# Running sums in two fp32r passes, ternary weights partly on ScalarE, gate steps on GpSimd, and new planner times

## The chip, the cores and the metric

The kernel runs on one core of one Trainium2 chip. The metric is the device time of one execution in microseconds. A core has TensorE (PE), VectorE (DVE), ScalarE (ACT), GpSimd (POOL) and a queue engine, SyncE (SP), which issues the DMAs here. Each engine executes its own instructions in order and waits on semaphores of the others.

## What is computed

Sixteen sequences of 256 tokens of width 256 pass through two layers; after each of the four steps stands `layernorm(x + step(x))`.

```python
# step 1: per head (16 heads of 16), Fourier transforms of q and kv, normalized,
#         kv summed up along the sequence
q, kv = x @ W_q.T, x @ W_kv.T
qf, kvf = l2norm(fft(q)), l2norm(fft(kv))
values = ifft(qf * cumsum(kvf, axis=sequence)).real @ W_o.T
# step 2: 8 experts; a gate per token picks one
x_diff = (x - mean_diff) / norm
score = (select_weight . x_diff)**2 summed over 8
gate = sigmoid(slope * (score - center)); scale = gate.max(); idx = gate.argmax()
mod = bias[idx] + degen[idx] @ (update[idx] . (x - debias[idx]))
out = (1 - scale) * x + scale * mod
# step 3: softmax attention, 16 heads of 16, W_qkv and W_o
# step 4: ternary weights, width 1024
def _ternary_weight(w, group_size):          # group_size = 64
    wb = w.astype(jnp.bfloat16)
    wg = wb.reshape(-1, group_size)
    scale = jnp.clip(jnp.mean(jnp.abs(wg), axis=-1, keepdims=True), 1e-08, None)
    q = jnp.clip(jnp.round(wg / scale), -1.0, 1.0)
    ...
h = square(relu(x @ ternary(W_fc).T)); out = rms_norm(h) @ ternary(W_proj).T
```

## The kernel before

The work is recorded first and ordered afterwards. Helpers `pe`, `dve`, `act`, `pool` and `op` (SP) record an operation with the tiles that it writes and reads, a cost in microseconds and a priority (`order.prio`, a virtual time: lower goes first). `Order.run` is a list scheduler: it keeps a clock for each engine, takes the engine whose next operation could start first, and of its operations that could start within `SLACK` of that the one with the lowest priority. Tiles get their buffers at that moment, so costs and priorities decide the order on every engine and which buffer is used when. `pin` fixes the order found. A DMA issue holds its queue for `ISSUE`.

The pieces of work are these.

- **Prologue.** `warm` and `fold_in` (L447, L459) prepare PE and the folded weights `wf`; `centred` (L505, L511) centres two weights on ScalarE; `fold_out` (L475 to L496) prepares `gi`, `ge`, `r0`, `r0b`.
- **front(b, early)**, steps 1 and 2 of sequence b, 16 times; sequences 0 to 3 are early. Projection (L645), squares and copies on ScalarE (L652, L653), sums (L656), an inverse root by three Newton steps on GpSimd (L664 to L667, four operations each), scaling (L671), transposes of q (L685) with a ScalarE copy (L689), the running sum of kv as a product with the triangle `tri` (L693, L694, output `cu`), products on VectorE (L700 to L702 early, L721 to L738 later), the inverse transform (L711 early, L747 later), layernorm (L586 to L599), transposes (L572, copied by L371 or L372), the gate's inputs (L768, L770, L779), and the gate: small operations of 16 columns, L792 to L809, in a chain over VectorE with the exponential on ScalarE (L798). `mk` (L812) is transposed (L823, L826) and multiplied with `dg` (L831); L838 and `layernorm_of_centred` (squares L612, root on GpSimd L580 and L581, scaling L617 or L620) give x2, whose transposes (L572) are copied to x2T.
- **ternaries()**: eight tiles of 128x512. Each is loaded, cast to bf16 (L526), reduced to sums of magnitudes per group of 64 (L527), and turned into signs times scale (L528 to L535, four of them 512 columns wide), all on VectorE but the cast; PE transposes it (L540) and a copy puts it in `w1T` or `w2T`. The tiles are held in `oT` and `o`, which the attention needs later (`terned`).
- **attention(i)**, step 3 for sequences 4i to 4i + 3 together, four times. Projections (L869) need x2T of all four; VectorE transposes them into `zt` (L878); some go to DRAM (L887) and back as `v` (L907). For 16 heads scores (L935) and their negated maxima (L944), transposed (L948, L949) and written back as a row (L952). Then, head by head, scores again (L974), exponentials (L983), values (L989), and for each pair of heads L997 to L1001 into `o`. Then transposes of `o` (L1018), the output product (L1032), sum (L1040) and layernorm.
- **back(b, late)**, step 4: transposes (L1054, L1057), split into high and low parts in fp32r (L1058), the first product (L1068), relu and squares (L1077 to L1086), split (L1090, L1092), the second product (L1100), norm (L1111, L1115), L1121, layernorm and the store.

The priorities interleave them: attention i stands around 100(i + 1), its maxima from -60 on, its heads from -10 on, 7 apart; fronts of the next group from 30 on, 15 apart; backs of the last group from 30 on, 20 apart. The last group's backs come at the end. An fp32 matmul stands in the trace as two records, an fp32r one as one.

## Time and profile before

| | |
|---|---|
| median of 3 runs | 754.0 us (742.52, 754.22, 754.0) |
| profiled execution | 740.27 us, of which the span of instructions is 738.5 |
| mean granted TensorE clock | 0.954 |
| PE, VectorE busy | 707.9, 619.4 us |
| ScalarE, GpSimd busy | 432.5, 186.3 us |
| first projection of an attention (L869) | at 87.4 us |

A profile line gives the line of the code, engine, operation, output and inputs with their shapes, the number of instructions, then busy time, mean time of one in ns, and idle time of the engine in front of them with what ended it. The records of one engine may overlap: the next operation starts before the last one's record ends, so the spacing of starts, not the length of a record, is what an operation costs in a row of them.

### The profile page before, as it was taken

What the parts mean: (1) busy time and instruction counts of PE and PEld (TensorE: products, weight loads), DVE (VectorE), ACT (ScalarE), POOL (GpSimd) and SP (SyncE); (2) the same over time, 40 slices, a digit from 0 to 9 for tenths busy, and PEclk for the clock granted to TensorE, in tenths of its full rate; (3) what the DMA queues carried; (4) which work ended last, traced back from release to release, by engine and by line L of the source; (5) the groups of instructions that cost most, each with busy time, mean ns of one, the idle gap of its engine ahead of it and who ended that gap; (6) DMA issues with size and microseconds to landing.
All of it is one profiled execution on the core that took longest, in us unless ns stands there. A gap on an engine that the chain in (4) does not pass through costs nothing.

```text
span 738.5 us, 15139 instructions
## 1 busy us (share of the span) xinstructions
PE 707.9 (96%) x5664; PEld 503.1 (68%) x5664; DVE 619.4 (84%) x1391; ACT 432.5 (59%) x929; POOL 186.3 (25%) x482
## 2 busy tenths in 40 slices
PE   9999898999999999999999999999989999999994
PEld 6687455765668567767755668787665677865993
DVE  2999997998788999899989879899559958784786
ACT  4436411344677246888571417879951278877883
POOL 3752011032415003335360014121110001120143
PEclk9999996798999999999999989999999989999996
DMA  9100102700101154010111403000001430000000
GB/s 292 64 30 30 28 11 73 60 23 8 32 16 29 32 81 59 16 36 21 34 45 33 64 3 31 1 17 16 17 15 30 69 31 16 17 17 16 1 30 29
DMA packets 86957, 27.16 MB, mean 37 GB/s; under 512 B 67996, under 2 KB 84196, under 8 KB 86884
## 3 DMA queue, kind: packets, MB, share of 16 engines
q1 hardware_dynamic: 86884, 26.20, 16.7%
q8 instruction: 44, 0.72, 0.4%
q14 instruction: 29, 0.24, 0.1%
HBM read 16.76 MB, written 8.91 MB: 35 GB/s over the span
## 4 chain that ended last, share of the span: by engine, by line
PE 70%; DVE 18%; POOL 4%; ACT 3%; issue 3%; DMA 1%; DVEq 0%; ACTq 0%
PE bank L869 10%; PE bank L935 9%; PE bank L989 8%; PE bank L974 8%; PE bank L1100 6%; PE bank L1068 6%; PE bank L645 5%; PE bank L1032 4%; DVE nm L944 4%; PE bank L747 2%; PE bank L572 2%; PE bank L831 2%; PE bank L693 1%; PE bank L770 1%; DVE zt L878 1%
## 5 line engine op out<-in xcount | busy, mean ns | idle before, releaser
L983 ACT ACTIVATE zt<-bank 128x512 f32<-128x512 f32 x256 | 134.3, 596 | 57.6 <-PE bank L974 45.3
L944 DVE TENSOR_REDUCE nm<-bank 128x2 f32<-128x512 f32 x256 | 158.3, 677 | 10.7 <-PE bank L935 10.4
L580 POOL TENSOR_SCALAR st<-st 128x2 f32<-128x2 f32 x80 | 24.3, 304 | 402.8 <-DVE st L1115 153.4
L869 PE MATMUL bank<-wqr,x2T 128*128 128x512 f32 (+1 forms) x256 | 91.8, 508 | 1.0 <-DVE nm L944 1.0
L935 PE MATMUL bank<-zt 16*128 16x256 f32 x1024 | 83.1, 424 | 1.6 <-ACT work L371 1.4
L974 PE MATMUL bank<-zt 17*128 17x256 f32 x1024 | 80.6, 409 | 1.3 <-DVE nm L944 0.7
L935 PEld LDWEIGHTS bank<-zt 16*128 16x128 f32 x1024 | 54.2, 196 | 31.5 <-issue 16.3
L869 PEld LDWEIGHTS bank<-wqr,x2T 128*128 128x128 f32 x256 | 48.5, 197 | 36.4 <-issue 28.8
L1068 PE MATMUL bank<-xs,w1T 128*128 128x256 f32 x512 | 72.5, 292 | 0.8 <-DVE xs L1058 0.5
L989 PE MATMUL bank<-zt,v 128*32 128x256 f32 x1024 | 72.7, 395 | 0.0
L878 DVE STREAM_TRANSPOSE zt<-bank 128x1024 f32<-128x1024 f32 (+1 forms) x48 | 66.5, 1462 | 7.2 <-PE bank L869 7.2
L1068 PEld LDWEIGHTS bank<-xs,w1T 128*128 128x128 f32 x512 | 65.8, 194 | 6.7 <-issue 2.7
L1100 PE MATMUL bank<-w2T,hi 128*128 128x256 f32 x256 | 69.1, 303 | 1.1 <-ACT hi L1090 0.9
L1100 PE MATMUL bank<-w2T,lo 128*128 128x256 f32 x256 | 65.5, 290 | 3.1 <-DVE lo L1092 3.1
L974 PEld LDWEIGHTS bank<-zt 17*128 17x128 f32 x1024 | 51.2, 188 | 22.0 <-issue 9.8
L581 POOL TENSOR_TENSOR st<-st,mhalf 128x2 f32<-128x2 f32 x80 | 62.5, 782 | 6.5
L645 PE MATMUL bank<-wf,x 128*128 128x512 f32 x128 | 63.2, 626 | 0.0
L371 ACT COPY work<-bank 128x512 f32<-128x512 f32 (+1 forms) x36 | 18.4, 515 | 62.3 <-PE bank L869 34.1
L1100 PEld LDWEIGHTS bank<-w2T,hi 128*128 128x128 f32 x256 | 49.7, 194 | 7.6 <-issue 3.9
L1092 DVE TENSOR_TENSOR lo<-work,hi 128x512 fp32r<-128x512 f32 x64 | 43.4, 682 | 13.1 <-ACT hi L1090 13.1
L1100 PEld LDWEIGHTS bank<-w2T,lo 128*128 128x128 f32 x256 | 49.9, 195 | 4.4 <-DVE lo L1092 4.1
L989 PEld LDWEIGHTS bank<-zt,v 128*32 128x32 f32 x1024 | 28.3, 111 | 31.9 <-issue 10.8
(205 smaller groups left out, 1261.3 us busy)
## 6 DMA issues: line engine op xcount, KB each, us to landing
x<-in_xT SPq DMA_DIRECT2D x16, 256.0 KB
v<-vd SPq DMA_DIRECT2D x32, 128.0 KB
out<-work SPq DMA_DIRECT2D x16, 256.0 KB
x<-in_x SPq DMA_DIRECT2D x12, 256.0 KB
vd<-work SPq DMA_DIRECT2D x12, 256.0 KB
vd<-work SPq DMA_DIRECT2D x12, 128.0 KB
oT<-in_wfc SPq DMA_DIRECT2D x4, 256.0 KB
o<-in_wproj SPq DMA_DIRECT2D x4, 256.0 KB
```

Of the source, the lines that this page charges most:

```text
L581: pool([dst], [dst, mhalf], 0.7, lambda: G.tensor_tensor(dst.v, dst.v, a(mhalf)[:, 0:n], ALU.pow))
L645: T.matmul(pb.v.rearrange("p a s k -> p (a s k)"), xT.v[:, c, ts(t, P)], a(wf)[:, c].rearrange("p a s f -> p (a s f)"), start=(c == 0), st ...
L869: T.matmul(b.v.rearrange("p j d -> p (j d)"), x2T.v[:, c, tb].rearrange("p g k -> p (g k)"), a(wqr)[:, c, j0 * HD : (j0 + nj) * HD], start ...
L878: lambda b=b, tb=tb, j0=j0, nj=nj: V.transpose(ztv[:, j0 : j0 + nj, ts(tb, 32)], b.v.unsqueeze(2).to_broadcast([P, nj, 2, HD])),
L935: T.matmul(sc[g].v[:, t, :], part(g, HD, 0, h, t * P, P), part(g, HD, 1, h), start=True, stop=True,)
L944: lambda nm=nm, sc=sc, g=g, k=k: V.tensor_reduce(nm.v[:, g, k, :], sc[g].v, AX.X, ALU.max, negate=True),
L974: T.matmul(sc[g].v[:, c, :], part(g, HD + 1, 1, h, c * P, P), part(g, HD + 1, 0, h), start=True, stop=True,)
L983: act([e], [sc[g]], 512, lambda e=e, sc=sc, g=g: A.activation(e.v, sc[g].v, AF.Exp, scale=HD ** -0.5))
L989: T.matmul(av.v[32 * g : 32 * g + 32, hk, :], v_part(g, h, c), es[g].v[:, c, :], start=(c == 0), stop=(c == 1),)
L1068: T.matmul(pb.v[:, i, :], a(w1T)[:, n // 2, ts(q * 2 + i, P)], xs.v[:, n % 2, n // 2, :], start=(n == 0), stop=(n == 3),)
L1092: dve([lo], [h, hi], 512, lambda h=h, hi=hi, lo=lo: V.tensor_tensor(lo.v, h.v, hi.v.bitcast(F32), ALU.subtract), us=0.63)
L1100: T.matmul(pw.v[:, t, :], part.v[:, i, ts(t, P)], a(w2T)[:, q * 2 + i, :], start=(q + t + i + n == 0), stop=(q + t + i + n == HID // P // ...
```

## The change

Line numbers behind the change are up to 22 higher.

- In later fronts the kv part is split into a high part in fp32r (`hi`, ScalarE) and the rest (`lo`, VectorE), and the running sum is the product of both with `trir`, an fp32r copy of the triangle: eight fp32r matmuls in place of four fp32 ones.
- For each ternary tile ScalarE takes magnitudes with their sums (8 operations of 64 columns), signs (512 columns) and signs times scale (8 of 64); VectorE compares magnitudes with the threshold and multiplies.
- Five gate steps go from VectorE to GpSimd in every front, a sixth in later ones.
- `ISSUE` goes from 0.43 to 0.6, the heads' spacing from 7 to 6, the backs' start from 30 to 45.

```diff
@@ -93,7 +93,7 @@
 NEAR = {PE: 0.0, DVE: 0.06, ACT: 0.06, POOL: 0.1, SP: 0.3}
 SLACK = {PE: 0.15, DVE: 0.1, ACT: 0.1, POOL: 0.1, SP: 0.0}
 SWITCH = 0.13
-ISSUE = 0.43
+ISSUE = 0.6
 MOVE = 1.2
 LATER = 15.0
 
@@ -393,10 +393,11 @@
     f0s = fixed(zt_[:, 3072:3360].rearrange("p (c f) -> p c f", c=2))
     rows = fixed(zt_[0:NE, 3360:3496])
     ge = fixed(zt_[:, 3496:4008].rearrange("p (m d) -> p m d", m=2))
-    ones, mhalf = const("ones", [P, P]), const("mhalf", [P, 2])
+    ones, mhalf, zero = const("ones", [P, P]), const("mhalf", [P, 2]), const("zero", [P, 1])
     wf = const("wf", [P, 2, 2, 2, P])
     gi = const("gi", [P, 2, D])
     r0 = const("r0", [P, 2, 136])
+    trir = fixed(place("trir", [P, S], F32R))
     r0b = const("r0b", [P, 136])
     dg = const("dg", [72, D])
     slope, center = const("slope", [P, NE]), const("center", [P, NE])
@@ -432,8 +433,10 @@
     load(lambda: a(wqr), wqkvT.rearrange("(c p) e -> p c e", p=P), wqr, prio=-8.0, size=3.0)
     load(lambda: a(wo1), wo1T.rearrange("(c p) e -> p c e", p=P), wo1, prio=-8.0)
 
+    act([trir], [small], 256, lambda: A.copy(a(trir), tri))
     dve([ones], [], P, lambda: V.memset(a(ones), 1.0))
     dve([mhalf], [], 2, lambda: V.memset(a(mhalf), -0.5))
+    dve([zero], [], 2, lambda: V.memset(a(zero), 0.0))
     va = [a(t)[:, 0 : H * GB * (HD + 1)].rearrange("p (n g d) -> p n g d", g=GB, d=HD + 1) for t in v]
     for t in v:
         pool([t], [], 1.2, lambda t=t: G.memset(a(t), 1.0))
@@ -516,7 +519,7 @@
         ng = 512 // GROUP
         w, up, dn = (tile_("tern", [P, ng, GROUP]) for _ in range(3))
         wb, sc = tile_("wb", [P, ng, GROUP]), tile_("sb", [P, ng])
-        tot, th = stat(ng), stat(2, ng)
+        tot, th, scf = stat(ng), stat(ng), stat(ng)
 
         def wide(t):
             return t.unsqueeze(2).to_broadcast([P, ng, GROUP])
@@ -524,15 +527,18 @@
         place_w = lambda: w.slot.ap if len(w_dram.shape) == 2 else w.slot.ap.rearrange("p (c f) -> p c f", c=2)
         op((SP, MOVE, lambda: nc.sync.dma_start(place_w(), w_dram)), [w], [], prio=-8.5)
         act([wb], [w], 512, lambda: A.copy(wb.v, w.v))
-        dve([tot], [wb], 512, lambda: V.tensor_reduce(tot.v, wb.v, AX.X, ALU.add, apply_absolute_value=True))
+
+        for g in range(ng):
+            act([(dn, g), (tot, g)], [wb], 76, lambda g=g: A.activation(dn.v[:, g], wb.v[:, g], AF.Abs, accum_out=tot.v[:, g : g + 1]))
+        act([up], [wb], 512, lambda: A.activation(up.v, wb.v, AF.Sign))
         dve([sc], [tot], 8, lambda: V.tensor_scalar(sc.v, tot.v, 1.0 / GROUP, TINY, ALU.mult, ALU.max))
 
-        dve([(th, 0)], [sc], 8, lambda: V.tensor_scalar(th.v[:, 0], sc.v, 257.0 / 512.0, None, ALU.mult))
-        dve([(th, 1)], [sc], 8, lambda: V.tensor_scalar(th.v[:, 1], sc.v, -257.0 / 512.0, None, ALU.mult))
-        dve([up], [wb, th], 512, lambda: V.tensor_tensor(up.v, wb.v, wide(th.v[:, 0]), ALU.is_gt), us=0.63)
-        dve([dn], [wb, th], 512, lambda: V.tensor_tensor(dn.v, wb.v, wide(th.v[:, 1]), ALU.is_lt), us=0.63)
-        dve([up], [up, dn], 512, lambda: V.tensor_tensor(up.v, up.v, dn.v, ALU.subtract), us=0.63)
-        dve([up], [up, sc], 512, lambda: V.tensor_tensor(up.v, up.v, wide(sc.v), ALU.mult), us=0.63)
+        dve([th], [sc], 8, lambda: V.tensor_scalar(th.v, sc.v, 257.0 / 512.0, None, ALU.mult))
+        dve([scf], [sc], 8, lambda: V.tensor_copy(scf.v, sc.v))
+        for g in range(ng):
+            act([(up, g)], [(up, g), scf, zero], 64, lambda g=g: A.activation(up.v[:, g], up.v[:, g], AF.Identity, bias=a(zero), scale=scf.v[:, g : g + 1]))
+        dve([dn], [dn, th], 512, lambda: V.tensor_tensor(dn.v, dn.v, wide(th.v), ALU.is_gt), us=0.63)
+        dve([up], [up, dn], 512, lambda: V.tensor_tensor(up.v, up.v, dn.v, ALU.mult), us=0.63)
         b = ps([P, 4, P], "p")
 
         def go():
@@ -679,6 +685,15 @@
 
         pq, cu = ps([P, 2, S], kind), ps([P, 2, S], kind)
 
+        kv = [] if early else [tile_("hi", [P, 2, 2, P]), tile_("lo", [P, 2, 2, P])]
+        for t in range(0 if early else 2):
+            k = lambda t=t: qk[t].v.rearrange("p a (s h) k -> p a s (h k)", s=2)[:, :, 1, :]
+            act([(kv[0], t)], [qk[t]], 256, lambda t=t, k=k: A.copy(kv[0].v[:, t], k()))
+            dve(
+                [(kv[1], t)], [qk[t], (kv[0], t)], 256,
+                lambda t=t, k=k: V.tensor_tensor(kv[1].v[:, t], k(), kv[0].v[:, t].bitcast(F32), ALU.subtract), us=0.4,
+            )
+
         def go():
             for e in range(2):
                 for t in range(2):
@@ -690,10 +705,14 @@
 
         def go():
             for e in range(2):
-                T.matmul(cu.v[:, e, :], part(0, e, 1), tri, start=True, stop=False)
-                T.matmul(cu.v[:, e, P:S], part(1, e, 1), tri[:, 0:P], start=False, stop=True)
-
-        pe([cu], [*qk, small, *extra], 1.28, go)
+                if early:
+                    T.matmul(cu.v[:, e, :], part(0, e, 1), tri, start=True, stop=False)
+                    T.matmul(cu.v[:, e, P:S], part(1, e, 1), tri[:, 0:P], start=False, stop=True)
+                for n, kn in enumerate(kv):
+                    T.matmul(cu.v[:, e, :], kn.v[:, 0, e, :], a(trir), start=(n == 0), stop=False)
+                    T.matmul(cu.v[:, e, P:S], kn.v[:, 1, e, :], a(trir)[:, 0:P], start=False, stop=(n == 1))
+
+        pe([cu], [*(qk if early else [*kv, trir]), small, *extra], 1.28 if early else 0.8, go)
         if early:
 
             one, two = w(P, 2, S), w(P, 2, S)
@@ -790,11 +809,14 @@
 
         num, z, gate, top, oh, first, keep = e16(), e16(), e16(), stat(2), e16(), stat(2), stat(2)
         dve([num], [c2], 128, lambda: V.tensor_reduce(num.v, c2.v.rearrange("p t (n s) -> p t n s", s=NR), AX.X, ALU.add))
-        dve([z], [f, x1sq], 16, lambda: V.tensor_tensor(z.v, f.v[:, :, 128:136], per_token(x1sq.v), ALU.add))
+        if early:
+            dve([z], [f, x1sq], 16, lambda: V.tensor_tensor(z.v, f.v[:, :, 128:136], per_token(x1sq.v), ALU.add))
+        else:
+            pool([z], [f, x1sq], 0.27, lambda: G.tensor_tensor(z.v, f.v[:, :, 128:136], per_token(x1sq.v), ALU.add))
         dve([z], [z], 80, lambda: V.reciprocal(z.v, z.v))
-        dve([z], [num, z], 16, lambda: V.tensor_tensor(z.v, num.v, z.v, ALU.mult))
-        dve([z], [z, center], 16, lambda: V.tensor_tensor(z.v, z.v, per_expert(a(center)), ALU.subtract))
-        dve([z], [z, slope], 16, lambda: V.tensor_tensor(z.v, z.v, per_expert(a(slope)), ALU.mult))
+        pool([z], [num, z], 0.27, lambda: G.tensor_tensor(z.v, num.v, z.v, ALU.mult))
+        pool([z], [z, center], 0.27, lambda: G.tensor_tensor(z.v, z.v, per_expert(a(center)), ALU.subtract))
+        pool([z], [z, slope], 0.27, lambda: G.tensor_tensor(z.v, z.v, per_expert(a(slope)), ALU.mult))
         act([gate], [z], 80, lambda: A.activation(gate.v, z.v, AF.Exp, scale=-1.0))
         dve([gate], [gate], 16, lambda: V.tensor_scalar(gate.v, gate.v, 1.0, None, ALU.add))
         dve([gate], [gate], 80, lambda: V.reciprocal(gate.v, gate.v))
@@ -804,9 +826,9 @@
         dve([oh], [oh, small], 16, lambda: V.tensor_tensor(oh.v, oh.v, per_expert(rev), ALU.mult))
         dve([first], [oh], 16, lambda: V.tensor_reduce(first.v, oh.v, AX.X, ALU.max))
         dve([oh], [oh, first], 16, lambda: V.tensor_tensor(oh.v, oh.v, per_token(first.v), ALU.is_equal))
-        dve([keep], [top], 2, lambda: V.tensor_scalar(keep.v, top.v, -1.0, 2.0, ALU.mult, ALU.add))
+        pool([keep], [top], 0.27, lambda: G.tensor_scalar(keep.v, top.v, -1.0, 2.0, ALU.mult, ALU.add))
         mk = tile_("mk", [P, 2, 72])
-        dve([mk], [oh, top], 16, lambda: V.tensor_tensor(mk.v[:, :, 64:72], oh.v, per_token(top.v), ALU.mult))
+        pool([mk], [oh, top], 0.27, lambda: G.tensor_tensor(mk.v[:, :, 64:72], oh.v, per_token(top.v), ALU.mult))
         dve(
             [mk], [mk, f], 128,
             lambda: V.tensor_tensor(
@@ -964,7 +986,7 @@
             for hk in range(2):
                 n = hp * 2 + hk
                 h = HEADS[n]
-                order.prio = base + -10.0 + 7.0 * n
+                order.prio = base + -10.0 + 6.0 * n
                 at = [z[q_at(h)], z[k_at(h)], turn[q_at(h)], turn[k_at(h)]]
                 sc = [ps([P, 2, S], "a") for _ in range(GB)]
 
@@ -1144,7 +1166,7 @@
         for g in range(GB):
             base = 100.0 * (i + 1)
             if i > 0:
-                order.prio = base + 30.0 + 20.0 * g
+                order.prio = base + 45.0 + 20.0 * g
                 back((i - 1) * GB + g, False)
             if i + 1 < NG:
                 order.prio = base + 30.0 + 15.0 * g
```

## The prediction

> **What bounds the kernel now.** I first read the page: busy time, slices, and the shares of the chain that ended last.
>
> ```profile
> span 738.5 us, 15139 instructions
> PE 707.9 (96%) x5664; PEld 503.1 (68%) x5664; DVE 619.4 (84%) x1391; ACT 432.5 (59%) x929; POOL 186.3 (25%) x482
> ...
> DVE  2999997998788999899989879899559958784786
> ACT  4436411344677246888571417879951278877883
> ...
> PE 70%; DVE 18%; POOL 4%; ACT 3%; issue 3%; DMA 1%; DVEq 0%; ACTq 0%
> ```
>
> PE at 96% looks like the bound, but its records overlap. The chain shows what a matmul takes when others queue behind it:
>
> ```profile
> 235.50 1.92 PE bank L1068 x16
> ...
> 54.91 1.73 PE bank L711 x8
> ```
>
> So a 256-column fp32r matmul takes 120 ns (its record says 292), and an fp32 one, which is two records, 2 x 216 = 433 ns. Counting every matmul this way gives about 602 us of PE work in the 738.5, not 708: some 18% of the span PE waits or runs below full clock. VectorE's 619 us hardly overlap, so VectorE is nearly as tight as PE. I then cut the span where the first attention's projections begin (L869 at 87.4 us), and where the last attention's values end:
>
> ```profile
> 0.00:87.40 87.40, 82.53 (x400) 60.54 (x401) 68.99 (x207) 43.29 (x102) 35.27 (x90) 0.98 0.29 94
> ...
> 87.40:678.00 590.60, 577.65 (x4930) 398.34 (x4928) 505.32 (x1092) 349.51 (x745) 133.47 (x360) 0.96 0.17 30
> 678.00:738.50 60.50, 47.67 (x338) 44.23 (x336) 45.04 (x93) 39.70 (x82) 17.53 (x32) 0.89 0.06 18
> ```
>
> (columns: stretch, length, busy PE, weight load, VectorE, ScalarE, GpSimd, then clock, DMA share, GB/s.) The prologue is bound by VectorE: after its first 12 us it is busy 9 tenths, ScalarE half. In the main stage VectorE is busy 86%. The tail (60 us) is the last four backs, which the change does not touch.
>
> **The change, part by part.** *Ternary weights*, 8 tiles, all in the prologue. The rows:
>
> ```profile
> L527 DVE TENSOR_REDUCE st<-wb 128x8 f32<-128x512 bf16 x8 | 5.4, 671 | 0.0
> L533 DVE TENSOR_TENSOR oT<-wb,st 128x512 f32<-128x512 bf16 x7 | 5.2, 737 | 0.0
> L535 DVE TENSOR_TENSOR oT<-oT,sb 128x512 f32<-128x512 f32 x5 | 3.4, 687 | 0.1
> L530 DVE TENSOR_SCALAR st<-sb 128x8 f32<-128x8 bf16 x8 | 1.7, 210 | 0.3
> ```
>
> VectorE loses per tile the sum of magnitudes (0.67) and two of its four wide operations (about 1.4): 2.1 us, 16.8 in all (one 8-column threshold becomes one copy). ScalarE gains per tile 8 magnitudes with a sum (64 columns each), one 512-column sign, and 8 scalings with two pointer operands. The trace has no such size; the spacing of starts is what counts:
>
> ```profile
> 71.28 0.42 ACT L612 ACTIVATE x<-work 128x256 f32<-128x256 f32 x1
> 71.60 0.18 ACT L612 ACTIVATION_READ_ACCUMULATOR x<-work 128x1 f32 x1
> 71.69 0.40 ACT L612 ACTIVATE x<-work 128x256 f32<-128x256 f32 x1
> ...
> 55.55 1.04 ACT L599 ACTIVATE work<-bank,st,st 128x256 f32<-128x256 f32 x2
> ```
>
> A 256-column square is followed after 0.32 us by its accumulator read, and that after 0.09 by the next one. A 256-column operation with two pointers is followed after 0.46 (1.04 less its own 0.58). Plain 512- and 256-column copies stand 0.49 and 0.31 apart, so a column is worth some 0.8 ns, and 64 columns cost 0.15 (magnitude) + 0.10 (read), and 0.30 (scaling). Per tile 8 x 0.25 + 0.5 + 8 x 0.30 = 4.9 us; eight tiles 39.4 us. The planner is told 0.165 and 0.154 for the small ones, together 3.1 us a tile, so ScalarE will run behind its plan. From below the price is bounded by L798 (16 columns, 0.10 to the next start), from above by whole records (L798's 0.22 and 48 columns more, 0.26, + 0.19; L599's 0.59 less 192 columns, 0.43): 23 to 60 us. Once, at the start, ScalarE also copies the triangle (0.31) and VectorE sets a zero column.
>
> [...]
>
> *What that does to the prologue.* ScalarE runs in order, and the first attention needs the fourth front's x2T, whose copy starts at 83.83. In the built order ScalarE's work up to that copy was 39.9 us by these spacings; now it is 82.1. Before 17.5 us it can do only 8.3 (it waits for PE and for the weights), so the copy ends at 9.2 + 82.1 = 91.3 at the earliest, against 84.4: the first attention starts at least 7 us later. At the latest: the tiles end on ScalarE near 88, and the fourth front's remaining chain is the 18 us that it took in this trace (L599 to x2T): 105, or 21 later. I take 11, nearer the low end, since ScalarE seldom waits once it is the late one, and since it includes about 1 us for the gate's new hops. The delay is not all lost: VectorE and PE use the time for fronts 4 to 6, which the new order puts before the first attention.
>
> *Gate steps.* Five per front (16 fronts), a sixth in the 12 later ones, leave VectorE:
>
> ```profile
> L793 DVE TENSOR_TENSOR st<-f,st 128x16 f32<-128x16 f32 x12 | 3.3, 272 | 0.7
> L795 DVE TENSOR_TENSOR st<-st,st 128x16 f32<-128x16 f32 x16 | 2.9, 182 | 0.5
> L590 POOL TENSOR_TENSOR st<-st,st 128x2 f32<-128x2 f32 x32 | 10.2, 318 | 2.3
> ```
>
> 12 x 0.27 + 16 x 0.87 = 17.2 us off VectorE. On GpSimd each costs 0.22 to 0.32 (L762, L590), 92 of them some 25 us; it is 25% busy, so that is hidden, but they queue behind Newton steps (12 of 0.33 per front) and GpSimd's squares. A front's chain grows by about 5 x 0.1 plus crossings of 0.1, some 1 us. Later fronts have that slack; without it each of 12 would cost 1 us.
>
> [...]
>
> *Running sums.* Per later front PE did 2 x 433 + 2 x 213 ns (L693, L694) = 1.28 us of fp32. Now it does 4 fp32r matmuls of 256 columns (0.48) and 4 of 128. A 128-column fp32r matmul is not in the trace: 60 ns if half of L1068's, 213 if no better than fp32. I take 108, the spacing of the 128-column transposes: 0.91, a saving of 0.37 x 12 = 4.4 us, with ends -0.6 and 6.7. In return VectorE gets 24 subtractions of 256 columns (0.42 by L1106): 10.1 us, ScalarE 24 copies (0.31): 7.4, hidden at 59% busy, though each puts two more hops in front of the running sum; uncovered, a front would wait about 1 us.
>
> *Order.* VectorE in all loses 16.8 + 17.2 - 10.1 = 24 us. The planner's new times (0.6 for a DMA issue, heads 6 apart rather than 7, backs from 45 on rather than 30) reorder nearly everything. SP issues the same DMAs; x loads, row loads and v loads change places in its queue, and an issue took 0.69 (L952, 2.77 for four) to 0.90 us (L907, 2.71 for three), so 0.6 is the nearer price; I count nothing for it. I summed work between the ends of the four attentions' values, in both built orders. VectorE (times 0.95, since summed records exceed busy time by 5%): before 112, 205, 86, 102; after 102, 161, 108, 114. PE: before 95, 189, 94, 106; after 95, 156, 104, 118. The larger of the two, added up: 517 before, 489 after. So the main stage has 20 us less VectorE and 10 less PE work, and 28 less where the limiting engine changes, because VectorE's heavy second stretch is evened out. At least 10 (PE alone), at most 31 (28 with the stage's stalls in proportion, 590.6/517); I take 28.
>
> *Sum.* 738.5 + 11 - 28 + 0 (tail) = 721.5; with the 1.8 us that lie around the span 723.3, against 740.27 for this execution. The runs shown are 742.52, 754.22 and 754.0; on the median's scale 754 x 723.3 / 740.27 = 737.
>
> **Rivals.** *No change that can be told* (2% is about what a measurement of this kernel can tell): main-stage gain 20 (VectorE's sum) or 10 (PE's), prologue 11 to 14. For: PE makes 70% of the chain. Against: 18% is VectorE, most of it L944. Net -9 to +4, on the median's scale 745 to 758, centre 749.
>
> *Slower, the prologue turned into a ScalarE bound.* Front 4's running sum now stands on PE ahead of the fourth front's last transposes, and its high part waits in ScalarE's queue, so both chains wait on one late queue. If the spacings are the full records (60 us), the copy ends near 112, 27 later; the main stage gives 10 back: +17, 771. It decides from about 25 us of delay on. For: the planner's price is too low by 1.8 us a tile. Against: ScalarE had 44 us idle there.
>
> *The fp32r passes do not pay* (128 columns at 213 ns): 5 us above the forecast, 742, in the middle of the range.
>
> **How the numbers follow.** Faster 0.40, no change 0.32, slower 0.28. The forecast's own range is 724 (gain 31, delay 7, order kinder by 7) to 739. The whole range reaches into the rivals: 716 to 772.
>
> **What would show it.** Right: the first L891 matmul at 95 to 101 us, not 87; ScalarE at 9 tenths from 18 to 90 us; 64-column magnitudes 0.25 apart with the read, scalings 0.30; VectorE near 595 us busy; from the first projection to the last attention's values about 563 us, not 591; a tail of 60. Wrong: the first projection beyond 108; or a main stage still over 580, with PE's waits for VectorE moved to ScalarE or GpSimd.

## The result, and the profile after

The changed kernel is slower: 770.35 us, median of 4 runs (770.16 to 772.25), against 749.31 for four runs of the kernel before beside it. The ratio is 1.036, with a 95% interval of 1.033 to 1.039. One program's executions differ with the clock they are granted (the kernel before: 742 us at 0.954, 754 us at 0.934), so every ratio here is taken over the faster executions of both kernels. The forecast of 737 was wrong in direction, and the time lies near the upper end of its range (716 to 772). The profiled execution took 770.27 us, its span is 768.5, so 30.0 more than before.

From the page of the changed kernel: span, busy time by engine, then VectorE, ScalarE and the granted TensorE clock in 40 slices of 19.2 us, and the shares of the chain that ended last. Behind them stands the clock row of the kernel before, in slices of 18.5 us.

```profile
span 768.5 us, 15361 instructions
...
PE 729.3 (95%) x5664; PEld 510.4 (66%) x5664; DVE 599.7 (78%) x1297; ACT 478.4 (62%) x1157; POOL 208.7 (27%) x574
...
DVE  2666689957977999998789998986769976732796
ACT  4999831244674158789851597857883258336784
...
PEclk9998979956999999999999999999999988658998
...
PE 70%; ACT 13%; DVE 12%; issue 2%; POOL 2%; DMA 1%; DVEq 0%; ACTq 0%; POOLq 0%
```

```profile
PEclk9999996798999999999999989999999989999996
```

VectorE lost 20 us, much as forecast (599.7 against 619.4; the forecast said 595). PE, which by the forecast's count has 4 us less work now, is busy 21 us longer (729.3 against 707.9). The clock row points to the reason: slices 8 and 9 (from 154 us) and 34 and 35 (from 653 us) stand at 5 and 6 tenths. The same three stages as before, cut at the first attention projection (now L891, at 111.5 us) and at the end of the last attention's values (columns as in the forecast's table of stages: stretch, length, PE, weight load, VectorE, ScalarE, GpSimd, clock, DMA share, GB/s):

```profile
0.00:111.50 111.50, 94.58 (x436) 69.22 (x437) 68.06 (x203) 85.97 (x311) 50.14 (x153) 0.92 0.24 76
111.50:709.30 597.80, 588.42 (x4892) 399.07 (x4891) 486.51 (x1002) 352.78 (x764) 141.10 (x389) 0.92 0.16 29
709.30:768.50 59.20, 46.31 (x339) 42.11 (x336) 45.09 (x93) 39.69 (x82) 17.48 (x32) 0.95 0.06 19
```

The prologue is 24.1 us longer, the main stage 7.2, the tail 1.3 shorter. But the clock in the main stage went from 0.96 to 0.92. I call "lost clock" the length of a span times (1 - mean granted clock): 34.0 us before (738.5 x 0.046), 59.2 after (768.5 x 0.077). The rest of the span is 704.5 before and 709.3 after. So by this bookkeeping 25 of the 30 us are lost clock, and 5 are everything else. What a microsecond of lost clock is worth in time, the runs with added matmuls show further down.

The two long half-clock stretches in the trace after, by the same columns; the part of the first one from 154.6 to 164.9, also at 0.50, is left out:

```profile
151.20:154.60 3.40, 3.40 (x35) 2.07 (x26) 3.23 (x10) 0.28 (x2) 0.33 (x2) 0.50 0.04 9
...
164.90:185.30 20.40, 20.40 (x136) 12.85 (x132) 12.19 (x27) 6.01 (x14) 6.43 (x19) 0.50 0.01 1
185.30:188.70 3.40, 3.40 (x25) 1.89 (x21) 1.31 (x3) 2.49 (x8) 0.00 (x0) 1.00 0.01 1
```

```profile
663.20:697.30 34.10, 34.10 (x247) 17.62 (x245) 15.53 (x31) 13.24 (x28) 1.29 (x4) 0.50 0.03 10
```

In both, PE has a matmul in flight all the time (20.40 of 20.40 and 34.10 of 34.10 us, at 0.50): it is not starved, it is slow. Both lie in attention, where scores use 16 or 17 of 128 rows (L957, L996) and values 32 of 128 columns (L1011).

### The profile page after: what moved, and what is told of

Its sections match the earlier page's. It is cut to its first block, busy times and chain, and to the rows that moved or that the text cites. A ratio compares the mean times of both kernels' runs of the same rounds, so it can differ in the third digit from the quotient of the medians.

```text
span 768.5 us, 15361 instructions
## 1 busy us (share of the span) xinstructions
PE 729.3 (95%) x5664; PEld 510.4 (66%) x5664; DVE 599.7 (78%) x1297; ACT 478.4 (62%) x1157; POOL 208.7 (27%) x574
## 4 chain that ended last, share of the span: by engine, by line
PE 70%; ACT 13%; DVE 12%; issue 2%; POOL 2%; DMA 1%; DVEq 0%; ACTq 0%; POOLq 0%
PE bank L891 11%; PE bank L996 10%; PE bank L1011 9%; PE bank L957 9%; PE bank L651 6%; PE bank L1090 4%; PE bank L1122 4%; PE bank L766 3%; DVE nm L966 3%; PE bank L1054 3%; ACT oT L539 2%; PE bank L578 2%; PE bank L853 2%; PE bank L789 2%; DVE lo L1114 1%
## 5 line engine op out<-in xcount | busy, mean ns | idle before, releaser
L996 PE MATMUL bank<-zt 17*128 17x256 f32 x1024 | 90.4, 451 | 0.6 <-DVE nm L966 0.6
L957 PE MATMUL bank<-zt 16*128 16x256 f32 x1024 | 87.6, 427 | 2.5 <-ACT work L371 1.7
L891 PE MATMUL bank<-wqr,x2T 128*128 128x512 f32 (+1 forms) x256 | 88.9, 494 | 0.0
L1011 PE MATMUL bank<-zt,v 128*32 128x256 f32 x1024 | 82.5, 432 | 0.0
L957 PEld LDWEIGHTS bank<-zt 16*128 16x128 f32 x1024 | 53.7, 196 | 36.5 <-issue 14.5
L996 PEld LDWEIGHTS bank<-zt 17*128 17x128 f32 x1024 | 57.1, 210 | 29.3 <-issue 13.8
L1090 PE MATMUL bank<-xs,w1T 128*128 128x256 f32 x512 | 72.7, 293 | 0.7 <-DVE xs L1080 0.3
L1090 PEld LDWEIGHTS bank<-xs,w1T 128*128 128x128 f32 x512 | 65.9, 196 | 5.1 <-issue 2.4
L891 PEld LDWEIGHTS bank<-wqr,x2T 128*128 128x128 f32 x256 | 46.7, 190 | 32.6 <-issue 26.9
L587 POOL TENSOR_TENSOR st<-st,mhalf 128x2 f32<-128x2 f32 x80 | 60.9, 763 | 6.4
L371 ACT COPY work<-bank 128x512 f32<-128x512 f32 (+1 forms) x32 | 16.2, 505 | 68.6 <-PE bank L891 51.6
L1011 PEld LDWEIGHTS bank<-zt,v 128*32 128x32 f32 x1024 | 30.3, 118 | 40.4 <-issue 21.0
L1122 PEld LDWEIGHTS bank<-w2T,hi 128*128 128x128 f32 x256 | 50.4, 197 | 8.8 <-issue 4.8
```

Of the source, the lines that this page charges most:

```text
L587: pool([dst], [dst, mhalf], 0.7, lambda: G.tensor_tensor(dst.v, dst.v, a(mhalf)[:, 0:n], ALU.pow))
L891: T.matmul(b.v.rearrange("p j d -> p (j d)"), x2T.v[:, c, tb].rearrange("p g k -> p (g k)"), a(wqr)[:, c, j0 * HD : (j0 + nj) * HD], start ...
L957: T.matmul(sc[g].v[:, t, :], part(g, HD, 0, h, t * P, P), part(g, HD, 1, h), start=True, stop=True,)
L996: T.matmul(sc[g].v[:, c, :], part(g, HD + 1, 1, h, c * P, P), part(g, HD + 1, 0, h), start=True, stop=True,)
L1011: T.matmul(av.v[32 * g : 32 * g + 32, hk, :], v_part(g, h, c), es[g].v[:, c, :], start=(c == 0), stop=(c == 1),)
L1090: T.matmul(pb.v[:, i, :], a(w1T)[:, n // 2, ts(q * 2 + i, P)], xs.v[:, n % 2, n // 2, :], start=(n == 0), stop=(n == 3),)
```

## The clock, window by window

All half-clock stretches in the 20 profiles of this case are whole numbers of windows of 3.413 us (170 stretches; the last one of each profile, which ends with the record, is left out): in the clock records the one from 83.55 us in the trace of before lasts 3.413 us, the one from 663.15 in the trace after 34.133, ten windows. The records of these two traces have two values, 0.50 and 1.00. For each window I added up the matmuls that started in it: their duration at full clock (by the spacings that the forecast used) times active rows x columns / (128 x 128), as a share of the window. Call it the dense share. The clock of the window that follows goes with it:

| dense share of a window | now half: next half / full | now full: next half / full |
|---|---|---|
| under 0.32 | 200 / 4 | 155 / 5 |
| 0.32 to 0.44 | 145 / 58 | 35 / 95 |
| 0.44 and more | 0 / 108 | 0 / 3555 |

No half-clock window of the traces before and after held more than 0.56, so the 0.44 behind which full clock always followed is about four fifths of that. Attention's small matmuls reach 0.17 to 0.35 at half clock (the windows from 663 to 697 in the trace after; nine of these ten were followed by half clock again); at full clock the same kind of windows reach about 0.5 to 0.7 in attention 0 and 0.3 to 0.55 in the last one (e5 below, 157 to 174 and 656 to 683 us), and there they hold it. So the mix ran in both states. Before the first long stretch of the trace after stands a thin window: the one at 147.7 had 0.35, and ten windows at half clock followed.

PE's busy share does not tell what follows: ten windows in a row with PE busy 100% stayed at half clock (from 663.2 in the trace after, 34.10 of 34.10 us). Over all profiles 430 half-clock windows had PE busy for 99% and more; 273 of them were followed by half clock, 157 by full clock. The share of the array in use tells the two apart by the table: at 0.44 and more, none of 108 half-clock windows was followed by half clock, under 0.32, 200 of 204; whether it is the very quantity that sets the clock, or one that goes along with it, no run settles.

## The experiments

For each run: the first projection, span and mean clock of its profiled execution, lost clock and the rest of that execution as defined above, then the median of its timed runs and the ratio to the kernel before, measured beside it (medians of 744.7 to 745.4 us in the rounds of e1 to e18), with its interval.

| run | edit | first proj. | span | clock | lost | rest | median | ratio |
|---|---|---|---|---|---|---|---|---|
| before | | 87.4 | 738.5 | 0.954 | 34.0 | 704.5 | 749.31 | 1 |
| after | | 111.5 | 768.5 | 0.923 | 59.2 | 709.3 | 770.35 | 1.036 [1.033, 1.039] |
| e1 | after, ternary on VectorE | 94.2 | 771.1 | 0.918 | 63.2 | 707.9 | 765.09 | 1.031 [1.023, 1.039] |
| e2 | after, old constants | 112.4 | 772.2 | 0.928 | 55.6 | 716.6 | 764.57 | 1.025 [1.018, 1.033] |
| e3 | after, 64 dense matmuls | 112.5 | 776.1 | 0.935 | 50.4 | 725.7 | 776.08 | 1.043 [1.037, 1.050] |
| e4 | after, measured prices | 89.9 | 751.1 | 0.945 | 41.3 | 709.8 | 746.84 | 0.995 [0.988, 1.002] |
| e5 | after, two bursts | 113.2 | 746.2 | 0.969 | 23.1 | 723.1 | 750.92 | 1.012 [1.004, 1.020] |
| e6 | before, ternary, measured prices | 88.4 | 749.6 | 0.943 | 42.7 | 706.9 | 751.31 | 1.012 [1.003, 1.021] |
| e7 | before, sums and gate | 94.5 | 754.4 | 0.941 | 44.5 | 709.9 | 754.67 | 1.017 [1.010, 1.024] |
| e8 | before, new constants | 87.8 | 742.9 | 0.945 | 40.9 | 702.0 | 744.31 | 1.000 [0.996, 1.004] |
| e9 | before, gate | 93.8 | 731.0 | 0.961 | 28.5 | 702.5 | 732.39 | 0.979 [0.972, 0.986] |
| e10 | before, sums | 87.5 | 769.6 | 0.914 | 66.2 | 703.4 | 770.99 | 1.026 [1.016, 1.037] |
| e11 | before, ternary, low prices | 104.2 | 741.7 | 0.954 | 34.1 | 707.6 | 742.35 | 0.996 [0.9925, 0.9995] |
| e12 | e4 without gate | 88.2 | 776.9 | 0.921 | 61.4 | 715.5 | 774.69 | 1.036 [1.028, 1.044] |
| e13 | e10, passes twice | 87.2 | 767.4 | 0.934 | 50.6 | 716.8 | 769.51 | 1.028 [1.020, 1.036] |
| e14 | after, passes twice | 116.5 | 774.5 | 0.933 | 51.9 | 722.6 | 779.55 | 1.042 [1.033, 1.051] |
| e15 | after without sums | 111.9 | 773.8 | 0.925 | 58.0 | 715.8 | 772.05 | 1.030 [1.020, 1.041] |
| e16 | e4 without sums | 90.3 | 735.5 | 0.964 | 26.5 | 709.0 | 737.34 | 0.988 [0.985, 0.991] |
| e17 | e10, two bursts | 85.6 | 752.7 | 0.947 | 39.9 | 712.8 | 754.81 | 1.011 [1.007, 1.016] |
| e18 | after, bursts elsewhere | 113.8 | 776.9 | 0.916 | 65.3 | 711.6 | 778.59 | 1.039 [1.029, 1.049] |

Read the column "rest": in the 14 orders without added matmuls it stays between 702 and 717 us, whatever moved. The column "lost" runs from 26 to 66. Over the 129 runs of these 14 orders that have their clock on record, a line through span against lost clock has slope 1.03, and the correlation is 0.93.

### Parts undone (e1, e2, e4)

e1 puts the ternary block of the kernel before back. e2 puts back `ISSUE = 0.43`, `7.0 * n` and `30.0 + 20.0 * g`. e4 changes two prices, which only the planner reads:

```diff
-            act([(dn, g), (tot, g)], [wb], 76, ...AF.Abs...
+            act([(dn, g), (tot, g)], [wb], 165, ...AF.Abs...
-            act([(up, g)], [(up, g), scf, zero], 64, ...AF.Identity...
+            act([(up, g)], [(up, g), scf, zero], 270, ...AF.Identity...
```

> The changed kernel with the ternary weights back on VectorE (signs, sums and scales as before), all else as changed. Theory: ScalarE's 41 us of small operations bind the prologue, so the first projection comes back from 111.5 to 85-95 us and the run to 742-756 us, unless PE's clock falls elsewhere; the main stage still shows stretches of half clock that the new order makes. Rival (the new order or the hops of the gate and the split hold the prologue up): the first projection stays beyond 104 us and the time above 762.

> The changed kernel with the planner's three old numbers (0.43, heads 7 apart, backs from 30 on). Theory: the prologue is ScalarE's matter and stays near 111 us (105-114); the long stretches of half clock (33 us around 170, 34 us around 680) come from the new order, so most of the 48 us of lost clock (time times one minus granted clock) of the main stage goes back to 20-30, and the time to 745-758. Rival (the half clock comes from the late prologue or from the split and the gate, not from the order): lost clock stays above 40 and the time above 763.

> The changed kernel with the planner told the measured spacing of the small ScalarE operations (0.24 and 0.33 instead of 0.165 and 0.154). Theory (ScalarE's work itself binds the prologue): the first projection stays at 100-112 us, since the work is the same. Rival (only the plan's order in the prologue is at fault): it comes to 88-98 us. The whole time then depends on the clock: 745 to 772.

e1 brought the first projection back to 94.2 us as my theory said, and the time hardly moved (765, the rival's number): the late prologue was there, and was not what cost the time. e2 came out as its rival said: 764.57, with 41.0 us of lost clock in the main stage. It still has two long half-clock stretches, 17.1 us from 157 and 27.3 us from 535, the second in another attention. e4's first projection came at 89.9, as its rival said, and not at 100 or later: ScalarE's added work fits if it is ordered by its price. e4 won 23.5 us (746.84), and I read that at first as the price of the late prologue: ScalarE does as much in the stretch from 18 to 90 us in both, and only the order differs. After, then e4:

```profile
18.00:90.00 72.00, 60.84 (x308) 44.97 (x307) 47.70 (x146) 68.51 (x274) 28.32 (x89) 0.95 0.12 40
```

```profile
18.00:90.00 72.00, 61.77 (x334) 46.76 (x332) 48.27 (x153) 68.38 (x274) 32.30 (x95) 0.96 0.12 41
```

For where the first projection stands that reading is right: 111.5 against 89.9. For the time it is not: e4's rest is 709.8, the changed kernel's 709.3. All of e4's gain is lost clock, 41 against 59 us. Over e4's four timed runs lost clock goes from 25 to 41 us, and the rest stays between 709 and 713.

### Single parts on the kernel before (e6 to e11)

Each is one part of the diff above, put alone on the kernel before; e6 takes ternary weights with e4's prices, e11 with the low ones, e7 running sums and gate together.

> The kernel before with one part of the change alone, ternary weights' signs, sums and scales on ScalarE, and the planner told what these operations take by the changed kernel's trace (0.24 and 0.33 us). Theory (the work itself fits beside the fronts if it is ordered by its true price): first feed-forward projection at 86 to 92 us, time 738 to 756. Rival (39 us of added ScalarE work delays the fronts wherever it is put): first projection at 100 or later, time over 758.

> The kernel before with ternary weights' signs, sums and scales on ScalarE alone, at the changed kernel's low prices; beside the run with the measured prices it differs in two numbers that the planner reads, not in the work. Theory (the price alone makes the prologue late): first projection at 100 to 114 us against 88.4 with the measured prices, time 752 to 772. Rival (only together with the other parts, or with the new constants, does the low price hurt): first projection under 95, time 740 to 755.

> The kernel before with the other two parts that move work: running sums in two exact passes and six gate steps on GpSimd, ternary weights and planner constants as before. Theory (these parts are not what made the change slow): first projection at 87 to 91 us, VectorE busy some 10 us less or about the same, time 735 to 758. Rival (two hops over GpSimd in the chain of each front slow the fronts, which then come late to attention): main stage longer by 10 us or more at an equal share of lost clock, time over 758.

> The kernel before with the new planner constants alone (what an issue costs 0.60 for 0.43, heads 6 apart for 7, output projections from 45 for 30). Theory (these push attention's small matmuls into stretches of their own, where the clock is lost): clock lost in the main stage 38 us or more against 25.6, time 752 or more, first projection within 2 us of 87.4. Rival (the constants are harmless; the order changes, not the work): time within 2% of the kernel before, 735 to 755, lost clock 20 to 35 us.

> The kernel before with the gate steps on GpSimd alone. Theory (GpSimd's hops stand in the chains of the first four fronts, and that is the 7 us by which the first projection came late where running sums and gate were changed together): first projection at 92 to 97 us against 87.4, time 746 to 760. Rival (the gate steps are harmless, the running sums' copies and subtractions of front 5 and later push into the prologue): first projection at 87 to 90, time 738 to 750.

> The kernel before with the running sums in two exact passes alone. Theory (TensorE is the bound, and the passes take 0.76 us a front of it where 1.28 were): first projection at 86 to 90 us, main stage less its lost clock 558 to 565 against 565.0, time 736 to 750, no change that can be told. Rival (ScalarE's copy and VectorE's subtraction in front of each running sum cost more than TensorE saves): first projection at 92 or later, or time over 752.

e6 and e11 are the cleanest pair: the same work, two numbers apart. The low prices made the first projection 16 us later, as expected, and the time no later (742 against 751, not the 752 to 772 of my theory). The stages of e11, then of e6:

```profile
0.00:104.20 104.20, 88.74 (x424) 65.27 (x425) 66.34 (x207) 83.43 (x306) 43.24 (x123) 0.95 0.24 79
104.20:681.20 577.00, 569.26 (x4906) 386.08 (x4904) 497.69 (x1071) 342.98 (x739) 119.16 (x327) 0.96 0.17 31
```

```profile
0.00:88.40 88.40, 79.75 (x393) 59.91 (x393) 54.89 (x180) 73.63 (x282) 31.83 (x90) 0.96 0.28 90
88.40:689.10 600.70, 589.15 (x4935) 397.66 (x4936) 510.17 (x1096) 354.59 (x766) 132.12 (x360) 0.95 0.17 30
```

While ScalarE makes the first projection wait, PE does 9 us of other work (88.74 against 79.75), and the main stage is shorter for it (577.0 against 600.7; 9.9 of that is lost clock). Rest: 707.6 and 706.9.

e8: the constants are harmless, 1.000, with 32.4 us of lost clock in the main stage; the theory (38 or more, and 752) fell. e9: the first projection came 6 us later, as expected, yet the kernel is 2.1% faster than before, the best of all, and 14 us under the expectation. e10 was the surprise: running sums alone cost 26 us, all of it lost clock (rest 703.4), against an expected 736 to 750. e7 ended inside its range, at 754.67, but its first projection came at 94.5, not at 87 to 91, as late as in e9: it is the gate's steps on GpSimd that stand in the prologue's chains. e6 came as expected (first projection 88.4, 751.31).

### Is it the running sums? (e12 to e16)

e12 is e4 with the gate on VectorE; e15 and e16 put the fp32 running sums back into the changed kernel and into e4. e13 and e14 do each front's two passes twice, all other engines in the same order:

```diff
-                for n, kn in enumerate(kv):
+                for n, kn in [*enumerate(kv), *enumerate(kv)]:
```

> The changed kernel with the planner told 0.24 and 0.33 us for the small ScalarE operations, and with the gate steps back on VectorE. Theory (with the price right, what is left is a prologue as early as before, VectorE relieved of 17 us and TensorE of 5): first projection at 85 to 90 us, time 732 to 746, at best 1% below the kernel before; TensorE is busy anyway. Rival (what VectorE gives up is worth what my forecast took it for, 20 to 28 us in the main stage): 710 to 728.

> The kernel before with the two exact passes, each front's passes done twice (the second time overwrites the first; 12 fronts x 8 matmuls more, some 9 us of TensorE); order and all other engines as in the run with the passes alone, which took 771 us. Theory (fp32 running sums were dense work that held the clock up inside attention, and the shorter passes are too thin for that): clock lost in the main stage 45 us or less against 58.0, time under 758, though work was added. Rival (the copies, subtractions and the other order are the cause): lost clock 52 to 64, time 774 to 782.

> The changed kernel with each later front's two passes done twice, all else as it is. Theory (thin running sums lose the clock): the half-clock stretch at 151 to 185 us, in which fronts run, shrinks to half or less, the one at 663 to 697, where no front runs, may stay; clock lost in the main stage under 38 us against 47.8, time 755 to 766. Rival (the order is the cause): 777 to 782.

> The changed kernel with running sums as before (fp32, no copies and subtractions), all else as changed, at the low prices. Theory (the running sums are the part that makes the change slow): clock lost in the main stage 34 us or less, time 732 to 752. Rival (every part or the new constants add some): 758 to 772.

> The same as the run before in this list, with the planner told 0.24 and 0.33 us for the small ScalarE operations. Theory (the late prologue does not matter, the clock does): within 10 us of that run whatever its first projection, 730 to 752, first projection at 92 to 97. Rival (the price was worth 20 us, as the run with measured prices seemed to show): 15 us or more below that run.

The idea was that fp32 sums are 1.28 us of dense work per front, of which the passes leave 0.92. In the trace before, a half-clock window that held one had a dense share of 0.41 and was the last of its stretch (134.8 us); in e10 one with the short passes had 0.31 and was not (141.7). Doing the passes twice did bring the lost clock down, from 66.2 to 50.6 and from 59.2 to 51.9, but PE's added work took that back: times of 769.51 and 779.55, both misses. In e13 the first stretch did shrink (23.9 us, 34.1 in e10), but in e14 it was the wrong one: the one with fronts in it got longer (37.5 us from 155, against 34.1), the late one, without fronts, shorter (20.5 against 34.1). So the runs do not bear the idea out. Nor is e15, without the new sums, faster than the changed kernel (772.05, against the 732 to 752 of my theory), while e16, two planner prices away, is 35 us faster. That is what e16's rival said; my theory had the two within 10 us. Of the 38.3 us between their profiled spans lost clock is 31.5 and the rest 6.8, so this is not the price of a late prologue either. No part alone explains the slow kernel: the sums cost the kernel before 26 us, and taking them out of the changed kernel wins nothing. e12, on paper the better version, came out at 774.69 against an expected 732 to 746, with one half-clock stretch of 44 us in the last attention:

```profile
660.90:705.30 44.40, 44.40 (x326) 24.22 (x322) 19.02 (x38) 17.88 (x36) 2.20 (x6) 0.50 0.03 8
```

### Dense work put in by hand (e3, e5, e17, e18)

e3 adds one dense matmul ahead of each head's scores. The others put twelve ahead of one head in two places (e5: attention 0 head 2 and attention 3 head 6):

```diff
                 def go(sc=sc, h=h, n=n):
+                    if (i, n) in ((0, 2), (3, 6)):
+                        for _ in range(12):
+                            T.matmul(
+                                sc[0].v.rearrange("p t s -> p (t s)"), a(w1T)[:, 0, 0:P], a(w1T)[:, 0, 0:512],
+                                start=True, stop=True,
+                            )
```

> The changed kernel, same order, with one dense fp32r matmul of 128x512 more in front of each head's second scores (64 of them, written to a bank that the scores then overwrite; 0.215 us each at full clock, 14 us of added PE work). Theory (the small matmuls of attention, 16 or 17 rows or 32 columns each, do not count as enough activity to win the clock back): the two long half-clock stretches become shorter than 12 us each, the lost clock of the main stage falls from 48 to under 30, and the time falls by 5 to 18 us in spite of the added work. Rival (the clock falls because PE waits for others, and comes back by itself when they are done): the stretches stay, and the time rises by 5 to 14 us.

> The changed kernel with 24 matmuls more: twelve full 128 x 128 x 512 matmuls ahead of the scores of one head of attention 0 (in the stretch 151 to 185 us) and twelve ahead of one head of attention 3 (in 663 to 697 us); what they write is overwritten by the scores, so nothing of the computation changes. Their own work is some 2.6 us for twelve at full clock and 5.1 at half. Theory (the mix of small score and value matmuls cannot win the full clock back by itself, and the lost clock costs time): both long half-clock stretches end within two windows of 3.4 us after the burst, the clock lost in the main stage falls from 47.8 us to under 33, and the time falls by 8 to 18 us against the changed kernel, to 753 to 762, though work was added. Rival (the half clock is only what is seen while TensorE waits for others): the stretches stay, or go without a gain, and the time is that of the changed kernel plus 5 to 10 us, 775 to 780.

> The kernel before with the two exact passes (771 us), and twelve full 128 x 128 x 512 matmuls ahead of the scores of attention 0, head 0 (130.7 us, in the half-clock stretch from 124.6 to 158.7) and of attention 3, head 10 (683.8, in 681.0 to 708.3); what they write is overwritten. Theory (the lost clock is the cause): both stretches end within two windows after the burst, the lost clock of the main stage falls from 58.0 to 45 us or less, and the time by 8 to 18 us, to 753 to 763. Rival: stretches stay, or time of 771 to 779.

> The changed kernel (770 us) with the same twelve matmuls twice, but ahead of attention 1, head 8 (308 us) and attention 2, head 12 (518 us), where TensorE stood at full clock. Theory: they win nothing there, both long half-clock stretches stay, and the time is 770 to 780. Rival (bursts help anywhere, by shifting the order or by keeping TensorE warm): 750 to 763, as with the bursts in the half-clock stretches.

e3: the first long stretch went, the second stayed and grew (47.8 us, 655 to 703), and the 64 matmuls cost more than the clock gave (rest 16.4 us longer than the changed kernel's, lost clock 8.8 shorter): 776.08, the rival's number. In the last attention one dense matmul a head was too little to bring the full clock back.

e5: with 24 matmuls more the changed kernel fell from 770.35 to 750.92 us, 2 us beyond the expected range. Its clock by slices:

```profile
PEclk9999879999999999999999999999989989999997
```

The 5s and 6s are gone. The two attentions concerned, from first to last head's scores, first in the trace after, then with the bursts:

```profile
147.00:232.00 85.00, 85.00 (x751) 50.84 (x747) 65.70 (x167) 48.99 (x112) 23.94 (x80) 0.80 0.14 27
614.00:706.00 92.00, 89.64 (x761) 58.39 (x760) 51.46 (x107) 50.71 (x99) 9.98 (x22) 0.72 0.12 19
```

```profile
149.00:221.50 72.50, 72.42 (x759) 44.78 (x755) 64.94 (x167) 48.52 (x111) 23.77 (x80) 1.00 0.18 32
603.00:682.50 79.50, 76.05 (x761) 51.83 (x764) 50.85 (x107) 49.90 (x98) 11.00 (x22) 0.94 0.14 22
```

Each is 12.5 us shorter, with the same work on VectorE and ScalarE and more on PE. In e5's whole trace VectorE, ScalarE and GpSimd, and PE but for the bursts, run the same operations on the same tiles in the same order as in the trace after, so this is no other order. The sixteen score matmuls of a head took 2.09 us in the half-clock stretch of the trace after and 1.15 behind a burst:

```profile
672.40 2.09 PE L996 MATMUL bank<-zt 17*128 17x256 f32 x16
```

```profile
154.56 3.01 PE L996 MATMUL bank<-w1T 128*128 128x512 f32 x12
157.50 1.15 PE L1002 MATMUL bank<-zt 17*128 17x256 f32 x16
```

The first burst takes 3.01 us, which is full clock (at half clock, in e17 below, one takes 4.82): in e5 both bursts come before the clock falls, and keep it from falling. The counterpart is e18 below, the same order without a burst at this place: there a window of dense share 0.44 is followed by one of 0.20, and the half clock begins; in e5 one of 0.45 is followed by the burst's, 0.89, and the clock stays full.

e17 puts the bursts into another slow order, e10, at that one's own stretches: 770.99 became 754.81, as expected. Here they stand in the half clock, and end it. Windows around the first burst, then the second burst, at 4.82 us, and the windows around it:

```profile
123.60:127.00 3.40, 3.40 (x26) 2.45 (x18) 3.40 (x7) 0.00 (x0) 0.00 (x0) 0.50 0.62 67
127.00:130.40 3.40, 3.40 (x8) 2.71 (x9) 3.40 (x7) 0.00 (x0) 0.00 (x0) 0.50 0.90 84
130.40:133.80 3.40, 3.16 (x35) 2.18 (x34) 0.43 (x1) 1.15 (x3) 0.00 (x0) 1.00 0.11 9
```

```profile
672.66 4.82 PE L989 MATMUL bank<-w1T 128*128 128x512 f32 x12
```

```profile
669.70:673.10 3.40, 3.40 (x25) 1.96 (x22) 1.03 (x4) 1.39 (x3) 0.90 (x2) 0.51 0.03 5
673.10:676.60 3.50, 3.50 (x9) 2.71 (x9) 0.88 (x5) 0.78 (x2) 1.30 (x4) 0.51 0.02 5
676.60:680.00 3.40, 3.40 (x44) 2.02 (x46) 0.27 (x1) 1.37 (x3) 0.00 (x0) 1.00 0.00 0
```

The window filled by dense matmuls (eight and nine records) is the last one at half clock, both times. e18 is the control: as many matmuls in the changed kernel, same order, at places that were at full clock and stayed there without them. It took 778.59 us, as expected, and both long stretches stayed, the first somewhat shorter:

```profile
PEclk9998879957999999999999999999989879658997
```

```profile
158.10:185.40 27.30, 27.26 (x178) 16.19 (x178) 17.96 (x39) 8.30 (x19) 7.45 (x24) 0.50 0.26 19
670.10:704.20 34.10, 34.10 (x251) 17.80 (x246) 15.62 (x31) 13.17 (x27) 1.29 (x4) 0.50 0.03 10
```

So it is where the bursts stand that counts: lost clock costs time, and is not a mark of waiting. It does not cost its full length. e5 lost 36 us less clock than the changed kernel and its span fell by 22.3; the 24 matmuls take some 6 us themselves (2.94 from the first start of a burst to the next start behind it, 0.245 each, more than the 0.215 of the expectations), so the clock gave about 28, a little over three quarters. In e17 it is about 23 of 26. At that price, by this estimate, the 25 us of lost clock are some 20 to 22 of the 30; the slope of 1.03 above also holds what else differs from order to order.

## Why the prediction was wrong, point by point

- **"VectorE is nearly as tight as PE", and the term of 28 us.** This step decided the forecast, and failed. VectorE did get its relief (599.7 us). The main stage without its lost clock went from 565.0 (590.6 - 25.6) to 550.0 (597.8 - 47.8), 15 us less, but the prologue without its lost clock grew by 17.3 (103.0 against 85.7): work on fronts that stood behind the first projection now stands ahead of it. With the tail (2 us longer without its lost clock) the net is a loss of 5. Against the sum of 721.5 the span is 47 us over: 13 in the main stage, 6 in the prologue, 2 in the tail, 25 to 26 in lost clock. e16 says it once more: VectorE 590.1 us busy, 29 less than before, rest 709.0 against 704.5. VectorE was not the limit; the larger of two engines' sums per attention was not the length of that stage. One reason stands in the trace of before: the 602 us of PE work were too few. At full clock, from one start to the next, a head's sixteen scores take 1.08 us and its sixteen values 1.00:

```profile
646.84 1.15 PE L935 MATMUL bank<-zt 16*128 16x256 f32 x16
647.92 1.07 PE L989 MATMUL bank<-zt,v 128*32 128x256 f32 x16
648.92 0.61 PE L1111 MATMUL bank<-ones,work 128*128 128x1 f32 x4
```

  With all matmuls counted by such spacings I get some 630 to 645 us, of a rest of 704.5: PE was tighter than VectorE by more than the forecast saw.
- **The prologue's 11 us** measured 24.1 (about 7 of it lost clock), beyond the upper bound of 21. The spacings were right: magnitudes 0.24 with their read (0.25 in the forecast), scalings 0.33 (0.30):

```profile
75.67 0.26 ACT L532 ACTIVATE o<-wb 128x64 f32<-128x64 bf16 x1
75.81 0.21 ACT L532 ACTIVATION_READ_ACCUMULATOR o<-wb 128x1 f32 x1
75.91 0.26 ACT L532 ACTIVATE o<-wb 128x64 f32<-128x64 bf16 x1
...
80.68 2.76 ACT L539 ACTIVATE oT<-oT,zero,st 128x64 f32<-128x64 f32 x8
```

  With 0.52 for a sign (L533), eight tiles come to 41 us by these spacings, 39.4 in the forecast. The tiles ended on ScalarE at 83.4 us, even before the 88 assumed; it was the remaining chain to x2T's copy, taken as 18 us from the trace of before, that took 27 (to 110.6); up to 5 of the 9 more are lost clock (5.1 us there, 0.4 before), the others stay open. In e4's order the first projection starts even before the last tile ends (89.9 and 90.5). But the larger error was the sign that I gave the term: a later first projection is not a later end (e11 against e6), as long as PE has fronts to do.
- **The sum left out the clock.** The table of stages showed 0.96 in the main stage, the text spoke of time "below full clock", and no term asked what the new order would do to it. It is 25 of the 30 us by the bookkeeping, some 20 to 22 by the price that the bursts show: a term that stood at nothing and was the largest.
- **The rival of 771 us** hit the number by luck, with the wrong mechanism. Its delay came (24 us), and on PE a later front's running sum did stand ahead of the last transposes (L713 waits 1.18 us for `lo`, first row below); its price for the delay was wrong. The rival with passes that do not pay did not occur: from a matmul of 128 columns (L713) to the next it is 0.06 us at full clock, the low end of the bounds, from one of 256 (L712) 0.17, more than the 0.12 assumed; a front's eight take 0.92 us (e10's expectation took 0.76), and the forecast said 0.91, because its two errors cancel:

```profile
108.73 0.33 PE L713 MATMUL bank<-trir,lo 128*128 128x128 f32 x1 [1.18 <-DVE lo L694]
108.90 0.33 PE L712 MATMUL bank<-trir,hi 128*128 128x256 f32 x1
109.07 0.22 PE L713 MATMUL bank<-trir,hi 128*128 128x128 f32 x1
109.13 0.33 PE L712 MATMUL bank<-trir,lo 128*128 128x256 f32 x1
```

- **Right:** VectorE's busy time, the tail (59.2), the passes on PE, and that the gate steps on GpSimd, at 195 to 379 ns each against 163 to 272, cost nothing that is seen at the end, though they bring the first projection 6 us later. Alone (e9) they go with the fastest version; 5.5 of its gain over the profile of before is lost clock, 2 is rest.
- **Two small sums** were off and decide nothing: 28 in proportion (590.6/517) is 32, not 31, and the terms given for 724 come to 722. The 0.8 ns a column stands, though not by the 0.49 and 0.31 given with it: in the trace of before ScalarE's copies of 512 columns stand 0.47 apart (L653), one of 256 is followed after 0.27 (L371).

What stays open: why one order has thin windows and the next has not. Parts do not add up (e10, e15, e16), and I know of no rule short of computing the dense share of each window in the finished order. The versions that beat both kernels, e9 by 2.1% and e16 by 1.2%, are the ones that lose 28.5 and 26.5 us of clock; nobody planned that, so their gain is luck.

## What to carry to other kernels

Look at the clock row of the page before the busy shares: here the span less its lost clock hardly moved (702 to 717 us), and what did move was the lost clock (26 to 66). Matmuls on few rows or columns (16 or 17 rows, 32 columns of 128) fell to half clock and stayed there although TensorE was never idle (34.10 of 34.10 us busy from 663.2 on). Twelve full-array matmuls at that place kept the full clock (e5) or brought it back (e17), and cost their own time elsewhere (e18). They were empty ones; moving useful dense work there was not tried. A planner's reordering is a change to the clock too (34.1 us lost in e11, 42.7 in e6, the same work in two orders), so two orders of the same work are compared by their rest and their lost clock apart.

## What the hardware showed that I had not expected

- In the profiles of this case the clock changed only at the borders of 3.413 us windows, and what went with the next window's clock is the share of the array in use: under 0.32 it fell or stayed down in 355 of 364 windows, at 0.44 and more it rose or stayed up in all 3663. At half clock TensorE's busy share did not tell them apart: at 99% and more, 273 windows were followed by half clock and 157 by full clock.
- Twelve matmuls of 128x128x512, 3.01 us at full clock, placed where the clock would fall, shortened the attention they stood in by 12.5 us, twice (e5). Placed inside a half-clock stretch, twelve ended it within two windows from the first of them (e17).
- A microsecond of lost clock cost about 0.8 to 0.9 us of span (e5, e17; an estimate from their spans and lost clock), not a whole one.
- An fp32r matmul of 256 columns took 0.17 us when one of 128 stood behind it (L712 before L713 in the trace after), and 0.12 in a row of its own kind (L1090 there).
